# First queries before the second batch's divisors, one set-up product moved, and shift and scale read from DRAM in a four-layer kernel

## The chip, the cores and the metric

The kernel runs on one core of one Trainium2 chip. The metric is the device time of one execution in microseconds (us), as the median of several runs; lower is better. Before the change it is 702.77 us (median of 6 runs, 702.45 to 706.2).

## The reference

The input x has 8 batches of 256 tokens of 256 features; a condition vector of 64 numbers belongs to each batch. Four layers follow one another, each added to its input:

```python
x = x + L0(x, cond)   # norm scaled by cond, 16-head attention, norm, SwiGLU of width 1024
x = x + L1(x, mask, cond)
x = x + L2(x, cond)   # quaternion rotation of the features
x = x + L3(x, cond)   # router, top 2 of 8 experts, each three matmuls 256-512-512-256

# L1, after its attention:
out = out @ Wo.T
xn  = out / sqrt(mean(out*out) + EPS) * rms_scale
mod = silu(cond) @ Wc.T + bc            # 8 x 512
shift, sc = split(mod, 2)
xn  = xn * (1 + sc) + shift
```

The change touches the condition's part of L1 (`mod`) and the order of the first rounds. All numbers are float32.

## The kernel before, in words

**Staging.** The kernel works batch by batch. An attention of one layer and one batch is four *blocks*: `Attention.scores` does eight matrix instructions into `s` (L988, one buffer of four PSUM banks, `ps_s` with `bufs=1`) and one exponential on ACT, `pe` (L990). So the scores of a block cannot start before the exponential of the block before has read `s`. `values` (L1001) multiplies the exponentials with the values. Blocks are taken from a fixed `queue`, first those of layer L0 for batches 0, 1 and 2, then L1 and L0 in turn. Between blocks, `run` puts *pieces*: projections, SwiGLU products, transposes. All of these write to the pool `ps_m` (function `bank`), which has three buffers.

**What sets the order.** TensorE, VectorE and ScalarE take their instructions in the order of the Python text (`manual_schedule`); in the first stage, up to the six rounds of `run("bbbbbb", ...)`, GpSimd does too. SyncE, which issues most transfers, and GpSimd in the later stages are ordered by a planner. So where a function is called in the text is where its instructions stand in each engine's queue.

**The start.** `first_norm(b)` (through `normed`) takes the sums of squares of a batch on ACT (L878), then eleven small VectorE operations for the reciprocal root (`rsqrt`, L619 to L624, the "divisors"), then scales the tokens (`xs`, L900, on ACT for batches 0 and 1). `first(b)` transposes `xs` on TensorE and applies the condition's scale and shift on VectorE (`conditioned`, L924, giving `xT`), then projects keys (`pk`, L932, copied by ACT to `kT`), queries (`pq`, L932, scaled by VectorE to `qz`, L946, two instructions) and values (`pv`, L954, copied by ACT to `va`, L957). `prepare_condition` (L692 to L696) and `prepare_router` (L750 to L758) are eight short VectorE instructions and one on ACT; the first of them, `keyseen` (L692), reads the mask `maskT`, which GpSimd's queue loads fourth, behind `WcT`, `bc_b` and `rs_b`. `set_up_condition` multiplies silu(cond) with `WcT` (`pmod`, L715) into `mod_all`, 8 batches on 8 partitions, and GpSimd writes that to the DRAM tile `mod_rows` (L719). `set_up_router` is one more small product (`pgconst`, L763).

**The set-up in the six rounds.** `second_step` is a generator that is advanced once at the end of each of rounds 1 to 5. It interleaves `set_up_rotation` with the third batch's `first_turned(3)` and the norm `n2` of batch 1. `first_turned` sends its reciprocal roots through DRAM (`rstd_rows`, L1063) and back on all partitions (`rb`, L1065), and VectorE multiplies by them (`xr`, L1071). `set_up_rotation` makes, in its four steps: `rotg` and `gall`; then `coef`, `pmc` (L833, `mod` once more, now with features on partitions, from `silu_c` and `WcT`), from it `mc` (L834, L835) and `scaled` (L839); then the products `phall` (L847) and `pshift` (L854) with their readers `hall` (L851) and `each` (L856); and last `pshg` (L862) and its copy `shg` (L863).

Of the kernel before, what the change touches and what calls it, by code (L numbers as in the profile page):

```python
# [12 lines left out]
ALU = mybir.AluOpType  # L13
# [3 lines left out]
P = 128  # L17
B, S, D = 8, 256, 256
# [3 lines left out]
E, M = 8, 512  # L22
KC = D // P
# [11 lines left out]
WROW = B3O + D  # L35

SMALL = dict(condT=B, qrT=4, sgT=1, affb=4 * KC, rms=KC, wg=KC * E, ggw=E, wgb=E, ggb=E,
             wg4=4 * E, rms4=4, bcc=2 * KC, rsc=KC)

SL = 256  # L40

# [452 lines left out]
def block_kernel(ctx: ExitStack, tc: tile.TileContext, a: dict, out: bass.AP):  # L494
    nc = tc.nc
# [57 lines left out]
    def scales():  # L553

        nc.vector.tensor_scalar(pbit, pidx, DH, None, ALU.bitwise_and)
        nc.vector.tensor_copy(pbitf, pbit)
        nc.vector.tensor_scalar(par[:, 0:1], pbitf, -0.25 / DH, 0.25, ALU.mult, ALU.add)
        nc.vector.tensor_scalar(par[:, 1:2], pbitf, 0.25 / DH, None, ALU.mult)
# [12 lines left out]
    part, at = {}, 0  # L571
# [118 lines left out]
    def prepare_condition():  # L690

        nc.vector.tensor_scalar(keyseen, maskT8[:, :, 0], -1.0, 1.0, ALU.mult, ALU.add)  # L692

        nc.scalar.activation(tanh_c, condT[0:C, :], AF.Tanh, scale=0.5)
        nc.vector.tensor_scalar(half_c, condT[0:C, :], 0.5, None, ALU.mult)
        nc.vector.scalar_tensor_tensor(silu_c, tanh_c, 1.0, half_c, ALU.add, ALU.mult)  # L696
# [15 lines left out]
    def set_up_condition():  # L712

        pm = bank("pmod", (B, 2 * D))
        nc.tensor.matmul(pm, silu_c, wcT, start=True, stop=True)  # L715
        mod = wt("oT", [B, 2 * D], "mod_all")
        nc.vector.tensor_tensor(mod, pm, bc_b, ALU.add)
        nc.vector.scalar_tensor_tensor(mod[:, D:], mod[:, D:], 1.0, rs_b, ALU.add, ALU.mult)
        nc.gpsimd.dma_start(out=mod_rows, in_=mod)  # L719
        yield 0.4  # L720

    def set_up_slots():
# [81 lines left out]
    def set_up_rotation():  # L804
        prepare_rotation()

        nc.vector.tensor_tensor(
            wg4s, part["wg4"].rearrange("p (j e) -> p j e", e=E),
            part["rms4"].unsqueeze(2).to_broadcast([P, 4, E]), ALU.mult,
        )  # L810
        for h in range(2):
            r = slice(h * C, (h + 1) * C)
            nc.vector.tensor_copy(rmine[r], rotg[r].rearrange("p j (k h) -> p k h j", h=2)[:, :, h, :])
        turned = work.tile([P, KC, 4, E], F32, tag="raw", bufs=2, name="turned")
        nc.vector.tensor_tensor(
            turned, rmine.unsqueeze(3).to_broadcast([P, KC, 4, E]),
            wg4s.unsqueeze(1).to_broadcast([P, KC, 4, E]), ALU.mult,
        )
        nc.vector.tensor_reduce(gall, turned.rearrange("p k j e -> p k e j"), AX.X, ALU.add)
        nc.vector.tensor_copy(wv1[:, :, D:], gall)  # L820

        nc.sync.dma_start(out=coef_row, in_=rotg[0:C].rearrange("c j i -> c (j i)"))
        rows_in = wt("x4", [P, C, 4, 4], "coef_in", 1)
        nc.sync.dma_start(
            out=rows_in.rearrange("p c j i -> p (c j i)"),
            in_=coef_row.rearrange("c w -> (c w)").partition_broadcast(P),
        )
        yield
        nc.gpsimd.tensor_copy(coef, rows_in.rearrange("p c j i -> p i j c"))

        pm = bank("pmc", (P, 2 * KC, B))
        for k in range(2 * KC):
            nc.tensor.matmul(pm[:, k, :], wcT[:, k * P : (k + 1) * P], silu_c, start=True, stop=True)  # L833
        nc.vector.tensor_tensor(mc, pm, part["bcc"].unsqueeze(2).to_broadcast([P, 2 * KC, B]), ALU.add)  # L834
        nc.vector.scalar_tensor_tensor(  # L835
            mc[:, KC:], mc[:, KC:], 1.0, part["rsc"].unsqueeze(2).to_broadcast([P, KC, B]), ALU.add, ALU.mult
        )
        scaled = wt("mod", [P, KC, B, E], "scaled")
        nc.vector.tensor_tensor(  # L839
            scaled, mc[:, KC:].unsqueeze(3).to_broadcast([P, KC, B, E]),  # L840
            gall.unsqueeze(2).to_broadcast([P, KC, B, E]), ALU.mult,
        )
        yield
        ph = bank("phall", (P, KC, B * E))
        for c in range(KC):
            for k in range(KC):
                nc.tensor.matmul(  # L847
                    ph[:, c, :], wo1n[:, k, c * P : (c + 1) * P], scaled[:, k].rearrange("p b e -> p (b e)"),
                    start=k == 0, stop=k == KC - 1,
                )  # L850
        nc.vector.tensor_copy(hall.rearrange("p k b e -> p k (b e)"), ph)  # L851
        ps = bank("pshift", (B, E))
        for k in range(KC):
            nc.tensor.matmul(ps, mc[:, k, :], gall[:, k, :], start=k == 0, stop=k == KC - 1)  # L854
        each = work.tile([B, B, E], F32, tag="r_each", bufs=1, name="each")
        nc.vector.tensor_tensor(  # L856
            each, ps.unsqueeze(1).to_broadcast([B, B, E]),
            ident[0:B, 0:B].unsqueeze(2).to_broadcast([B, B, E]), ALU.mult,
        )
        yield  # L860
        pb = bank("pshg", (P, B * E))
        nc.tensor.matmul(pb, ones[0:B, :], each.rearrange("p b e -> p (b e)"), start=True, stop=True)  # L862
        nc.vector.tensor_copy(shg.rearrange("p b e -> p (b e)"), pb)  # L863
        yield
# [5 lines left out]
    def bank(name, shape=(P, 2, S)):  # L870
        return ps_m.tile(list(shape), F32, tag="m", name=name)
# [165 lines left out]
    def do(parts):  # L1037
        for _ in parts:
            pass
# [5 lines left out]
    def first_norm(b):  # L1045
        s = state[b]
        s["x"] = xs_in.pop(b)
        yield from normed(
            lambda xs: s.update(xs1=xs), s["x"], f"n1_{b}", nc.gpsimd if b > 1 else nc.scalar,
            (nc.scalar, nc.scalar if b else nc.vector),  # L1050
        )
# [700 lines left out]
    def chain(*gens):  # L1752
        for g in gens:
            yield from g
# [33 lines left out]
    def once(f, *args):  # L1788
        f(*args)
        yield  # L1790

    def at_once(*gens):
        for g in gens:
            for _ in g:
                pass
        yield
# [10 lines left out]
    with tc.manual_schedule(engines=by_text):  # L1807
        unread = ps_o.tile([P, P], F32, tag="o", name="unread")
        keep_busy(9)
        n1 = first_norm(0)  # L1810
        next(n1)
        next(n1)
        set_up_factors(0)
        set_up_factors(2)
        do(n1)
        keep_busy(3)
        g0 = first(0)
        next(g0)
        keep_busy(2)
        scales()  # L1820
        n1 = first_norm(1)
        next(n1)
        next(n1)
        next(g0)
        next(g0)
        do(n1)
        do(g0)
        blank = set_up_slots()
        prepare_condition()
        cond_g = prepare_router()  # L1830
        finish_slots(*blank)
        def third(b):

            operand = first(b)
            yield next(operand)
            yield from set_up_router(cond_g)
            yield from operand

        def take(n, pieces):
            for _ in range(n):  # L1840
                yield next(pieces)


        operands = first(1)
        run("b", chain(take(1, operands), set_up_condition(), set_up_router(cond_g)), 9.0, rest=False)
        run("b", take(1, operands), 9.0, {0: [once(prepare_quaternions)]}, rest=False)
        n1 = first_norm(2)
        run("b", iter(()), 0.0, {0: [n1]})
        run("b", operands, 9.0, {0: [at_once(n1)]}, rest=False)
        operands = first(2)  # L1850
        then = run("b", iter(()), 0.0, hold=True)
        run("b", take(1, operands), 9.0, owed=then, soon=1, rest=False)

        def second_step():
            rotation = set_up_rotation()
            next(rotation)
            yield
            n1 = first_turned(3)
            next(n1)
            yield  # L1860
            n2 = in_parts(1, "n2")
            next(n1)
            next(n2)
            next(rotation)
            yield
            do(n1)
            next(n2)
            next(rotation)
            set_up_ones()
            yield  # L1870
            do(n2)
            yield from rotation

        set_up = second_step()
        gaps = [1.9, 5.0, 7.2, 7.2, 7.2, 7.2]
        run("bbbbbb", chain(operands, others(0)), gaps, {n: [set_up] for n in range(1, 6)}, soon=2)
    by_text = {mybir.EngineType.DVE, mybir.EngineType.Activation}
    text_order = ctx.enter_context(ExitStack())
    text_order.enter_context(tc.manual_schedule(engines=by_text))
# [231 lines left out]
```

## Time and profile before

| what | value |
|---|---|
| median of 6 runs | 702.77 us |
| profiled execution | 703.18 us |
| its span on the core | 701.4 us |
| granted TensorE clock, mean | 0.995 |
| PE busy | 687.2 us, 98% |
| DVE busy | 365.8 us, 52% |
| ACT busy | 255.5 us, 36% |
| POOL busy | 180.3 us, 26% |
| DMA, slices 0 to 2 of 40 | 8, 4 and 1 tenths busy |

PE is TensorE, DVE VectorE, ACT ScalarE, POOL GpSimd, SP SyncE. The profile is one execution; its time lies 1.8 us above its span. The first two of forty slices (17.5 us each) are the only early ones in which the transfers fill the queues: the weights of the first layers arrive there. A chain of waits, followed back from the last instruction, names at each time the work that set the end.

### The profile page before, as it was taken

To read this page: it belongs to the slowest core of one execution; us is meant where nothing else is said; L and a number is where in the kernel's file an instruction comes from. 1 tells how busy PE (TensorE), PEld (TensorE's weight loads), DVE (VectorE), ACT (ScalarE), POOL (GpSimd) and SP (SyncE) were. 2 spreads that over 40 slices of the span, in tenths; PEclk is the share of its full clock that TensorE was granted. 3 is DMA by queue.
4 is the path that set the end of the run, shared out by engine and by line. 5 is a ranking of instruction groups with operands and counts; after the bars stand their busy time and mean duration, and the time that the engine had idled before them with its cause. 6 is when DMAs were issued, how large, how long until landed. Compare 5 with 4: busy or idle time off the path is not lost.

```text
span 701.4 us, 11187 instructions
## 1 busy us (share of the span) xinstructions
PE 687.2 (98%) x4258; PEld 530.8 (76%) x4258; DVE 365.8 (52%) x1165; ACT 255.5 (36%) x411; POOL 180.3 (26%) x223
## 2 busy tenths in 40 slices
PE   8999999999999999999999999999999999999995
PEld 7567776767667667766666786688888998999894
DVE  4664354584488576477675676688222222222221
ACT  4664243544454444354443235332111222221220
POOL 5501500000000231000320016224373432443213
PEclk9999999999999999999999999999999999999998
DMA  8410201002011001020000051746595866676712
GB/s 301 152 61 17 38 1 38 16 1 39 16 61 39 1 17 8 6 71 1 9 9 1 17 204 18 301 139 208 145 312 158 231 238 180 174 268 195 250 24 29
DMA packets 28879, 70.01 MB, mean 100 GB/s; under 512 B 9033, under 2 KB 22225, under 8 KB 26385
## 3 DMA queue, kind: packets, MB, share of 16 engines
q1 hardware_dynamic: 20032, 57.70, 25.2%
q0 software_dynamic: 8496, 11.32, 7.4%
q8 instruction: 35, 0.57, 0.3%
q14 instruction: 28, 0.22, 0.1%
q10 hardware_dynamic: 288, 0.18, 0.1%
HBM read 59.67 MB, written 9.53 MB: 99 GB/s over the span
## 4 chain that ended last, share of the span: by engine, by line
PE 90%; DVE 5%; ACT 2%; DMA 1%; issue 1%; SPq 0%; POOL 0%; POOLq 0%; DVEq 0%; ACTq 0%
PE ph_a_rest L1528 10%; PE s_a L988 9%; PE pd L1141 8%; PE pg L1128 8%; PE ph_a_p L1528 7%; PE ph L1128 7%; PE o_a L1001 7%; PE ph_s_sure L1528 6%; PE pe_a_rest L1558 3%; PE pq_a L932 3%; PE pk_a L932 3%; PE pe_a_p L1558 3%; PE py L1024 2%; PE pe_s_sure L1558 2%; PE pv_a L954 2%; PE py L1174 2%
## 5 line engine op out<-in xcount | busy, mean ns | idle before, releaser
L990 ACT ACTIVATE pe_a<-s_a 128x2048 f32<-128x2048 f32 x64 | 120.1, 1876 | 101.0 <-PE s_a L988 100.9
L988 PE MATMUL s_a<-qz_a,kT_a 32*128 32x512 f32 x512 | 73.0, 640 | 3.0 <-DVE xg L1159 0.9
L1001 PE MATMUL o_a<-pe_a,va 128*32 128x256 f32 x1024 | 61.9, 382 | 0.0
L1128 PE MATMUL pg<-xT_n,gate_wT 128*128 128x256 f32 x256 | 61.8, 385 | 0.0
L1128 PE MATMUL ph<-xT_n,hid_wT 128*128 128x256 f32 x256 | 61.6, 384 | 0.0
L1001 PEld LDWEIGHTS o_a<-pe_a,va 128*32 128x32 f32 x1024 | 30.0, 110 | 39.8 <-issue 23.4
L1141 PE MATMUL pd<-out_wT,hT 128*128 128x256 f32 x256 | 59.7, 385 | 0.4 <-DVE hT L1136 0.4
L1141 PEld LDWEIGHTS pd<-out_wT,hT 128*128 128x128 f32 x256 | 47.4, 190 | 13.7 <-issue 4.0
L1128 PEld LDWEIGHTS ph<-xT_n,hid_wT 128*128 128x128 f32 x256 | 47.7, 190 | 13.2 <-DVE rq_v_n L619 2.3
L1128 PEld LDWEIGHTS pg<-xT_n,gate_wT 128*128 128x128 f32 x256 | 47.6, 190 | 11.9 <-issue 3.6
L1010 DVE STREAM_TRANSPOSE tu_a<-o_a 128x512 f32<-128x512 f32 x32 | 22.8, 712 | 52.3 <-PE o_a L1001 52.3
L1528 PE MATMUL ph_a_rest<-h_a_rest,w_a_rest 128*128 128x256 f32 x224 | 49.6, 380 | 0.0
L1528 PEld LDWEIGHTS ph_a_rest<-h_a_rest,w_a_rest 128*128 128x128 f32 x224 | 42.1, 190 | 5.4
L1101 POOL TENSOR_TENSOR xy<-y,x 128x512 f32<-128x512 f32 x8 | 10.1, 1268 | 139.3 <-DVE rq_v_r L619 55.0
L1539 DVE TENSOR_SCALAR h_a_rest<-ph_a_rest,w_a_rest 128x256 f32<-128x256 f32 x28 | 13.5, 484 | 57.3 <-PE ph_a_rest L1528 56.3
L1316 POOL DMA_INDIRECT slots<-rec,posi x32 | 31.8, 994 | 22.1 <-issue 7.6
L988 PEld LDWEIGHTS s_a<-qz_a,kT_a 32*128 32x128 f32 x512 | 20.1, 183 | 22.2 <-issue 13.1
L1134 DVE SCALAR_TENSOR_TENSOR sg<-th,pg 128x512 f32<-128x512 f32 x32 | 21.9, 685 | 28.4 <-ACT th L1132 28.3
L1528 PE MATMUL ph_a_p<-h_a_p,w_a_p 128*128 128x192 f32 (+2 forms) x224 | 36.0, 319 | 0.0
L1132 ACT ACTIVATE th<-pg 128x512 f32<-128x512 f32 x32 | 19.0, 594 | 46.4 <-PE pg L1128 46.4
L1537 ACT ACTIVATE h_a_rest<-ph_a_rest,w_a_rest 128x256 f32<-128x256 f32 x28 | 13.2, 473 | 60.7 <-DVE h_a_rest L1539 60.7
L1528 PEld LDWEIGHTS ph_a_p<-h_a_p,w_a_p 128*128 128x128 f32 x224 | 34.9, 191 | 0.1
(351 smaller groups left out, 1177.7 us busy)
## 6 DMA issues: line engine op xcount, KB each, us to landing
w_a_rest<-in_experts SPq DMA_DIRECT2D x7, 2180.0 KB, 9.5
w_a_p<-in_experts SPq DMA_DIRECT2D x7, 2180.0 KB, 9.2
w_s_sure<-in_experts SPq DMA_DIRECT2D x4, 2180.0 KB, 10.1
w_s_early<-in_experts SPq DMA_DIRECT2D x1, 2180.0 KB
mod<-mod_rows SPq DMA_DIRECT2D x8, 256.0 KB, 3.3
tokens<-x SPq DMA_DIRECT2D x4, 512.0 KB, 3.8
out<-x SPq DMA_DIRECT2D x4, 512.0 KB, 4.9
x<-in_x SPq DMA_DIRECT2D x7, 256.0 KB, 2.7
```

The lines of the kernel that those rows point to most:

```text
L932: nc.tensor.matmul(pp[:, c, :], w[:, k, c * P : (c + 1) * P], xT[:, k, :], start=k == 0, stop=k == KC - 1)
L988: nc.tensor.matmul(sc[:, j], kT[r, c, kc * P : (kc + 1) * P], qz[r, c], start=True, stop=True)
L990: nc.scalar.activation(pe, sc, AF.Exp)
L1001: nc.tensor.matmul(o[32 * i : 32 * i + 32, qd, :], va[:, kc, 8 * c + 4 * qd + i].rearrange("p a d -> p (a d)"), pe[:, 2 * qd + i // 2, i % ...
L1010: nc.vector.transpose(turned.rearrange("p q j a d -> p (q j a d)"), o.rearrange("p q s -> p (q s)"))
L1128: nc.tensor.matmul(ps[:, j, :], w[:, k, o : o + P], yT[:, k, :], start=k == 0, stop=k == KC - 1)
L1132: nc.scalar.activation(th, pg, AF.Tanh, scale=0.5)
L1134: nc.vector.scalar_tensor_tensor(sg, th, 1.0, pg, ALU.add, ALU.mult)
L1141: nc.tensor.matmul(pd[:, t, :], hT[:, c, t * P : (t + 1) * P], out_w[:, c, :], start=c == 0, stop=c == HID // P - 1)
L1316: sc = nc.gpsimd.indirect_dma_start(out=slots, out_offset=bass.IndirectOffsetOnAxis(ap=posi[:, t : t + 1], axis=0), in_=rec[:, t, :], in_o ...
L1528: nc.tensor.matmul(ph[:, c - c0, 0:many], w[:, o : o + P], src[:, k, 0:many], start=k == 0, stop=k == n_in - 1,)
L1558: nc.tensor.matmul(pos[q][0:p, q, :], h2[:, k, q * p : (q + 1) * p], w[:, o : o + D], start=k == 0, stop=k == MC - 1,)
```

## The change

Three edits, all before the steady rounds:

```diff
 SMALL = dict(..., wg4=4 * E, rms4=4
-             , bcc=2 * KC, rsc=KC)
+             )
...
 def set_up_condition():
...
         nc.gpsimd.dma_start(out=mod_rows, in_=mod)
+
+        for j in range(2 * KC):
+            nc.sync.dma_start(out=mc[:, j, :], in_=mod_rows[:, j * P : (j + 1) * P].rearrange("b p -> p b"))
         yield 0.4
...
 def set_up_rotation():
...
-        pm = bank("pmc", (P, 2 * KC, B))
-        for k in range(2 * KC):
-            nc.tensor.matmul(pm[:, k, :], wcT[:, k * P : (k + 1) * P], silu_c, start=True, stop=True)
-        nc.vector.tensor_tensor(mc, pm, part["bcc"]..., ALU.add)
-        nc.vector.scalar_tensor_tensor(mc[:, KC:], mc[:, KC:], 1.0, part["rsc"]..., ALU.add, ALU.mult)
         scaled = wt("mod", [P, KC, B, E], "scaled")
...
         scales()
+        prepare_condition()
+        cond_g = prepare_router()
         n1 = first_norm(1)
-        next(n1)
         next(n1)
         next(g0)
         next(g0)
-        do(n1)
+        next(n1)
         do(g0)
         blank = set_up_slots()
-        prepare_condition()
-        cond_g = prepare_router()
         finish_slots(*blank)
...
-        run("b", chain(take(1, operands), set_up_condition(), set_up_router(cond_g)), 9.0, rest=False)
-        run("b", take(1, operands), 9.0, {0: [once(prepare_quaternions)]}, rest=False)
+        run("b", chain(set_up_condition(), set_up_router(cond_g)), 9.0, {0: [at_once(n1)]}, rest=False)
+        run("b", take(2, operands), 9.0, {0: [once(prepare_quaternions)]}, rest=False)
...
         def second_step():
...
             next(rotation)
             set_up_ones()
             yield
+            next(rotation)
+            yield
             do(n2)
-            yield from rotation
...
-        run("bbbbbb", ..., {n: [set_up] for n in range(1, 6)}, soon=2)
+        run("bbbbbb", ..., {n: [set_up] for n in range(1, 6)}, soon=2, starts={5: [set_up]})
```

First, the eight small VectorE instructions of the condition and the router come ahead of everything of batch 1, and batch 0's `qz` comes ahead of batch 1's eleven divisors. Batch 1's `xs` moves behind the first block, and its transposes, `xT` and `pk` stand together between the second and the third block; before, the transposes and `xT` stood between the first and the second. Second, `pmc` and its two VectorE readers are gone; four transfers by SyncE fill `mc`, each reading 128 features of all 8 batches from `mod_rows`, single 4-byte numbers that lie 2 KB apart, to 128 partitions. Third, `pshg` and `shg` stand at the start of round 5, right behind that round's scores, and no longer at its end; `n2`'s last step stays at the end.

## The prediction

> **What bounds the kernel.** I read the page first: engine shares and the chain that ended last.
>
> ```profile
> PE 687.2 (98%) x4258; PEld 530.8 (76%) x4258; DVE 365.8 (52%) x1165; ACT 255.5 (36%) x411; POOL 180.3 (26%) x223
> ...
> PE 90%; DVE 5%; ACT 2%; DMA 1%; issue 1%; SPq 0%; POOL 0%; POOLq 0%; DVEq 0%; ACTq 0%
> ```
>
> TensorE sets the time. Of its 14 us of idling, some 7 lie behind its last matmul; the view of waits finds about 5 us before that, 3 of them in the first 90 us, where all three edits lie. So a microsecond won or lost there should arrive at the end whole: behind 92 us the chain is PE almost throughout. Next I read the chain of waits in order of time up to 140 us (start, duration, what).
>
> ```profile
> 11.13 0.52 ACT junk_n L878 x2
> ...
> 13.81 1.32 DVE qz_a L946 x2
> 15.13 0.07 DVE keyseen L692
> ...
> 15.28 1.17 PE s_a L988 x8
> 16.45 0.02 issue
> 16.47 1.89 ACT pe_a L990
> 18.36 0.04 issue
> 18.40 1.19 PE s_a L988 x8
> ...
> 64.27 0.99 PE pmc L833 x8
> ...
> 76.13 0.18 PE pshift L854 x4
> 76.31 1.07 PE s_a L988 x8
> ...
> 82.76 0.36 PE pshg L862 x2
> 83.12 0.60 PE pt_x L888 x4
> 83.72 0.02 issue
> 83.74 0.59 ACT x2T L1154
> ```
>
> Up to 15.28 the chain runs over batch 1's squares and divisors to batch 0's `qz`: that is what the first edit attacks. Then scores and exponential alternate every 3.13 us (15.28, 18.40, 21.54, 24.68). `pmc` stands in the chain with 0.99, and behind `pshg` the chain leaves PE for `x2T`. Last, the timeline, for what the chain does not name.
>
> ```profile
> 5.06 0.77 POOL L525 DMA_DIRECT2D maskT<-in_maskT  x1
> ...
> 11.04 1.89 PE L932 MATMUL pq_a<-xT_n,L_WqT 128*128 128x256 f32 x8
> ...
> 17.04 1.00 DVE L924 TENSOR_SCALAR xT_n<-pt_n,aff 128x256 f32<-128x256 f32 x2 [0.60 <-PE pt_n L888]
> ...
> 74.76 0.69 DVE L1071 TENSOR_TENSOR xr<-xr,rb 128x512 f32<-128x512 f32 x1 [3.92 <-DMA rb<-rstd_rows]
> ...
> 78.02 0.20 DVE L856 TENSOR_TENSOR each<-pshift,ident 8x64 f32<-8x64 f32 x1
> ```
>
> **Edit 1, the start.** `pq` ends at 11.04 + 1.89 = 12.93, so `qz` can start at 12.98 where it started at 13.73. Its two instructions take 1.40, to 14.38. PE has `pv` until about 14.5 (its 12.76 start plus the usual 1.73), so the first scores go at 14.50, not 15.28: 0.78 won. The eight small instructions, 15.05 to 16.10 in the trace or 1.05 in all, move into the idle 2.03 us that DVE had before the divisors, behind 9.64; they are hidden if `maskT` has landed by 12.98 - 1.05 = 11.9. Its landing is not shown. `bc_b`, the same queue's load two ahead, landed 4.7 us after its issue, which gives 9.8; the slowest of that queue's early transfers (`out<-zero`, 256 KB) took 6.7, which gives 11.8. I take 9.8, the nearest row, and nothing for it. `keyseen` ran unheld at 15.05, so that is the ceiling.
>
> Now what comes behind. Scores 14.50, exponential 15.69 to 17.58, second scores 17.62: still 0.78 ahead. In between PE has only `pmod` and `pgconst` (1.02 + 0.43). The divisors run 14.4 to 16.5, and `xs` (0.91 on ACT) behind the exponential, to 18.5, under the second scores. Before, transposes and `xT` were done under the first exponential, and `pk` (19.47, 1.93 to the next PE work) filled the second. Now all three stand behind the second scores: transposes at 17.62 + 1.07 = 18.69, first half of `xT` 0.69 later (16.35 to 17.04 in the trace) and 0.55 long, `pk` at 19.98. PE idles 0.7 there and about as long before the second scores. Third scores at 19.98 + 1.93 = 21.91, fourth at 25.04, against 24.68: **0.4 us lost**. If `pk` needs both halves of `xT`, 0.8. If `pk` should not hold the third scores, 0.8 is won. I take 0.4: batch 0's `pk` started at 9.20, when only one half (8.60 to 9.15) was done.
>
> **Edit 2, `mc`.** `pmc` leaves PE: **-0.99**, the chain's row. The two DVE instructions (0.18 + 0.17) lay in DVE time that now becomes waiting: nothing. Added are four SP transfers, at the trace's 0.32 to 0.47 an issue. They wait for `mod_rows`, which the first load of `mod` (26.12) waited for too; with its DVE producers 0.5 later, say 26.6. Queued behind them on SP are that load (read at 84.87) and batch 3's `x` and `xT` (38.15 and 38.63, waiting for a buffer): nothing is late as long as the four end before 38. 4096 pieces of 4 bytes have no like here. Below: a `trec` load, 256 pieces of 16 bytes, landed in 1.8 us at best, so 16 times that in a row is 29 us, landing by 56. Above: `rb`, 128 pieces, took 4.3 us; its engines were busy about 2.6 us for 8 pieces each (0.33 us a piece), which for 256 each is 84 us, landing near 111. The `trec` row is nearest in size. `scaled` is due at 67.7, so I take nothing; the lower bound is hidden with 11 us to spare, the upper is not.
>
> A rule speaks against this edit. The Trainium skill, "DMA: Bandwidth & Descriptors", section "Rules for kernel authors", says that a non-contiguous last dimension becomes one descriptor per element, and puts a rearranged plain transfer at 19 times a hardware transpose. As an estimate from that page, 19 times the 3.3 us in which a `mod` load landed is 63 us, a landing near 89 and some 22 us lost; by the `trec` row the sum has no such term, and I follow the row.
>
> **Edit 3, `pshg`.** Its 0.36 is the same in either place, but it needs `each`. DVE reaches `each` only behind `xr` (held to 74.76 by `rb`), eleven divisors and `hall`: done at 78.22, 78.27 on PE. PE without `pmc` stands at `pshg` at 77.38 - 0.99 = 76.39: **a new wait of +1.9**. `rb` starts from divisors that follow PE's `pg` ahead of `pmc`, so the whole chain shifts with edit 1 and 1.9 holds. Behind it wait the last quarter of `pd`, then `pk`, `pq`: all of PE. In return, `pv` no longer stands behind `pshg` and `pt_x`: of three `ps_m` buffers, `pshg` held one there; now `pk`'s is free. From `pt_x` to `pv` it was 1.26, elsewhere transposes take 0.44 to the next PE work (88.10 to 88.54): **-0.8**. If `pv` waits as before, 0; if `each` came in time, the +1.9 would be 0.
>
> A rule again: "TensorE: Matmul & The Clock Gate", Part 1, has the clock halve after an idle window of about 3.4 us. The row is the granted clock, 1.00 in every 2 us up to 100, also where PE idled 0.6 of 2 us. By the rule 1.9 us alone would cost nothing; one of 3.4 us would, and the sum would gain about 1.7.
>
> **Sum:** +0.4 - 1.0 + 1.9 - 0.8 = **+0.5 us**. On the profiled execution: span 701.4 to 701.9, time 703.2 to 703.7. On the median, 0.4 below that execution: 702.77 + 0.5 = **703.3 us**, no change that can be told: 0.3% (2.1 us) is about what a measurement of this kernel can tell from none.
>
> **Rivals.**
> *The mask holds the queries* (slower). From a landing at 11.9 on, every microsecond delays `qz`. Against: both neighbours of that load say 9.8 to 11.8. For: transfers fill the queues up to 24 us. At the ceiling `keyseen` runs at 15.05, `qz` ends at 17.5, first scores 17.55, and the same steps bring the fourth to 28.1: 3.4 lost, not 0.4. That is 706.3.
> *`mc` late* (slower). From 67.7 on DVE stands at `scaled`, and `tu`, `hT` and so `pd` behind it. A landing at 72 costs 72 - 67.7, some 4 us: 707.6; at the upper bound of 111 it would be 43, or 746, to which I give no more than 0.02. The `rb` row speaks for it, the `trec` row against.
> *The lead stays and nothing stalls* (faster). `pk` does not hold the third scores and `each` comes in time: -0.8 - 1.0 - 0.8 = -2.6, 700.2. Against: the text order of DVE, which puts `xr` ahead of `each`. Without the stall alone: +0.5 - 1.9, 701.4.
> *The queues are planned anew.* SP everywhere and POOL in the later stages are not in text order, and three buffers of `ps_m` are dealt out afresh. For: POOL's `xT_n` (1.1 for two) waited 41.1 us in all behind others. If in three rounds it stands behind one more `xs` of 1.27, 3.8 is lost: 707.1. Gains are bounded by the few microseconds of PE waits left: a case of -2.5, 700.8 with the sum.
>
> **Chances.** Forecast 0.46; no stall alone 0.08 (both within). Mask 0.12, of which 0.08 beyond 0.3%. `mc` 0.08, of which 0.06 beyond. Lead kept 0.07, faster. Queues 0.19, of which 0.13 slower and 0.06 faster. In all: faster 0.13, same 0.60, slower 0.27. **Range** 700.8 to 706.6: the mask's ceiling, the single lost stall and part of the queues; about 0.1 stays out on each side. The forecast's own range is 702.1 to 704.5 (`pv` not gained +0.8, both halves +0.4; upper sizes of the gains below).
>
> **What would show it.** Right: first scores near 14.5, `keyseen` not waiting; `pk` of batch 1 behind the second scores with PE idle 0.6 before it, fourth scores near 25.0; no `pmc`; `mc` landed before 56 and no wait at `scaled`; PE waiting about 1.9 for `each` ahead of `pshg`; `pv` 0.44 behind `pt_x`; from 92 on the same steps some 0.5 later. Wrong: `keyseen` held by a transfer, DVE held at `scaled`, no wait at `pshg`, or a difference that appears behind 92 us.

## The result and the profile after

| | before | after |
|---|---|---|
| median | 703.24 us (67 runs, 702.19 to 706.63) | 707.51 us (30 runs, 704.03 to 713.55) |
| profiled execution | 703.18 us | 710.14 us |
| its span | 701.4 us | 708.4 us |

The changed kernel is slower: ratio 1.0058, with a 95% interval of 1.0045 to 1.0072. Forecast were 703.3 us and a range of 700.8 to 706.6, so the median lies 0.9 us above the range. One thing must be known before the spans are compared: in some executions of the kernel before, and of most others here, the matrix work of the first 12 us runs at half pace, which makes an execution some 3.3 us longer; the profile after is of such an execution and the one before is not, so what follows compares steps and not spans.

TensorE sets the end of the changed kernel as it did before. From its page, the engines' busy time and their shares of the chain:

```profile
PE 692.8 (98%) x4250; PEld 535.1 (76%) x4250; DVE 365.7 (52%) x1163; ACT 255.4 (36%) x411; POOL 180.2 (25%) x223
...
PE 90%; DVE 6%; ACT 1%; DMA 1%; issue 1%; POOL 0%; POOLq 0%; DVEq 0%; ACTq 0%
```

Eight matrix instructions fewer (`pmc`), yet PE is busy 5.6 us longer. Work that is less and takes longer has been slowed, so the durations in the chain are the next thing to read. The chain of waits of the changed kernel (start, duration, what):

```profile
5.71 3.51 PE paff L636 x16
...
12.50 2.59 PE pk_a L927 x8
15.10 1.73 PE pq_a L927 x8
...
18.55 1.11 PE s_a L983 x8
...
21.62 1.14 PE s_a L983 x8
22.76 0.60 PE pt_n L883 x4
23.38 0.56 DVE xT_n L919
23.98 2.01 PE pk_a L927 x8
26.00 1.11 PE s_a L983 x8
...
29.06 1.14 PE s_a L983 x8
...
74.91 4.30 DMA rb<-rstd_rows
79.23 0.69 DVE xr L1066
...
82.57 0.13 DVE each L851
82.75 0.69 PE pshg L857 x2
83.43 3.71 PE pd L1136 x8
87.14 2.81 PE pk_a L927 x8
89.96 1.73 PE pq_a L927 x8
91.69 0.44 PE pt_x L883 x4
92.12 1.73 PE pv_a L949 x8
```

Three things are to be seen. `paff` takes 3.51 us at the start (1.88 in a trace with the start alone, further down): the half pace of the first 12 us, which has nothing to do with the change. Behind the second scores stand `pt_n`, `xT_n` and `pk` in one row, as forecast. And behind `pshg` eight `pd` products take 3.71 us and eight `pk` products 2.81. In the chain before, the same products, and `pv`, took:

```profile
77.38 1.93 PE pd L1141 x8
79.30 1.73 PE pk_a L932 x8
...
84.38 1.99 PE pv_a L954 x8
```

The view of PE's waits names one new one, its cost in total, count and longest:

```profile
PE pshg L857 <- DVE each L851: 2.0, 1, 2.0
```

The windows of 2 us of the changed kernel give, behind the window and its length, the busy time and instructions of each engine (PE, PEld for its weight loads, DVE, ACT, POOL), then the granted TensorE clock, the DMA share and GB/s:

```profile
80.00:82.00 2.00, 0.78 (x8) 0.00 (x0) 1.70 (x9) 1.16 (x1) 1.90 (x3) 1.00 0.55 120
82.00:84.00 2.00, 1.25 (x4) 1.04 (x5) 0.87 (x5) 0.72 (x1) 1.90 (x3) 0.60 0.53 142
84.00:86.00 2.00, 2.00 (x6) 1.64 (x5) 0.00 (x0) 0.00 (x0) 2.00 (x2) 0.50 0.00 0
86.00:88.00 2.00, 2.00 (x6) 1.56 (x5) 0.69 (x1) 0.00 (x0) 1.91 (x3) 0.50 0.00 0
88.00:90.00 2.00, 2.00 (x7) 1.64 (x7) 0.00 (x0) 0.00 (x1) 2.00 (x2) 0.70 0.02 4
90.00:92.00 2.00, 2.00 (x13) 1.76 (x12) 0.28 (x1) 1.38 (x3) 0.61 (x1) 1.00 0.00 0
```

In shorter windows the granted clock falls to 0.50 at 82.4, while PE still waits, and is back at 89.2: six products in 2 us instead of eleven. In the trace before it is 1.00 in all of these windows. The 7.0 us between the spans are then, from the steps of the two chains:

| step | us |
|---|---|
| `pq` starts at 15.10, not 11.04 (half pace, not of the change) | +4.1 |
| `pq` to fourth scores: 13.96, not 13.64 | +0.3 |
| fourth scores to the place of `pmc`: 39.60, not 39.59 | 0.0 |
| `pmc` gone | -1.0 |
| wait for `each` | +2.0 |
| `pshg`, `pd`, `pk` at half clock: 7.21, not 0.36 + 1.93 + 1.73 | +3.2 |
| `pt_x` to the end of `pv`: 0.44 + 1.73, not 1.26 + 1.99 | -1.1 |
| behind that | -0.5 |

The row "behind that" is 608.95 us from the scores near 99 to the end, against 609.43 before; in ten traces, these two and eight of the runs below, it lies between 608.9 and 609.7, so nothing of the change is seen there.

### The profile page after: what moved, and what is told of

Same layout as the page of the kernel before. It is cut to its first block, busy times and chain, and to the rows that moved or that the text cites. A ratio compares the mean times of both kernels' runs of the same rounds, so it can differ in the third digit from the quotient of the medians.

```text
span 708.4 us, 11172 instructions
## 1 busy us (share of the span) xinstructions
PE 692.8 (98%) x4250; PEld 535.1 (76%) x4250; DVE 365.7 (52%) x1163; ACT 255.4 (36%) x411; POOL 180.2 (25%) x223
## 2 busy tenths in 40 slices
DMA packets 33039, 70.02 MB, mean 99 GB/s; under 512 B 13193, under 2 KB 26385, under 8 KB 30545
## 4 chain that ended last, share of the span: by engine, by line
PE 90%; DVE 6%; ACT 1%; DMA 1%; issue 1%; POOL 0%; POOLq 0%; DVEq 0%
PE ph_a_rest L1523 10%; PE s_a L983 9%; PE pg L1123 8%; PE ph_a_p L1523 7%; PE pd L1136 7%; PE o_a L996 7%; PE ph L1123 7%; PE ph_s_sure L1523 6%; PE pk_a L927 4%; PE pq_a L927 3%; PE pe_a_rest L1553 3%; PE pe_a_p L1553 3%; PE pv_a L949 2%; PE py L1019 2%; PE pe_s_sure L1553 2%; PE py L1169 2%
## 5 line engine op out<-in xcount | busy, mean ns | idle before, releaser
L1136 PE MATMUL pd<-out_wT,hT 128*128 128x256 f32 x256 | 61.5, 392 | 0.4 <-DVE hT L1131 0.4
```

The lines of the kernel that those rows point to most:

```text
L1136: nc.tensor.matmul(pd[:, t, :], hT[:, c, t * P : (t + 1) * P], out_w[:, c, :], start=c == 0, stop=c == HID // P - 1)
```

## The experiments

My theory was now that the first two edits do what was worked out, and that the third costs its wait and, on top of it, a stretch of half clock. Rivals: the start costs more than 0.4 to 0.5 (its new gaps lower the clock, or the half-paced start comes more often), `mc` costs something, or it is chance. The four kernels of the first set are compared with 35 runs of the kernel before, median 703.09 us, on the same chip.

**The whole change without its third edit.** `pshg` is back at the end of round 5.

```diff
-            next(rotation)
-            yield
             do(n2)
+            yield from rotation
...
-        run("bbbbbb", ..., soon=2, starts={5: [set_up]})
+        run("bbbbbb", ..., soon=2)
```

> The changed kernel with pshg put back to the end of round 5 (edit 3 undone; edits 1 and 2 stay). Theory, the clock: the loss of some 4 us is the 2.0 us wait for each and the half clock that follows it (pshg, pd and pk together 7.2 us instead of 4.0), so both go: before + 0.5 (start) - 1.0 (pmc), about 0.5 us below before, and granted clock 1.00 from 70 to 100 us. Rival, the start: edit 1 makes the first 12 us run at half pace (paff 3.5 us instead of 1.95 in the profile of the changed kernel), 3.3 us; then this run stays about 3 us above before.

Measured: 703.35 us, ratio 1.0003 (0.9981 to 1.0025). The clock is 1.00 in every window from 80 to 88 and the mean granted clock of its runs 0.9965, as before; after the change it is 0.9928 on average. So the loss goes with the third edit; the interval leaves 1.3 us below to 1.8 us above before. The gain of 0.5 that the other two should leave is not seen in the median, nor excluded. Part of the reason stands in its chain: `pk` behind `pd` starts at 82.50, when `each` is done, and takes 1.97, not 1.73. It reads nothing of `each`; the link that the source offers is a `ps_m` buffer, which `pshift` holds until `each` has read it. `each` delays PE also where `pshg` doesn't wait for it.

**The first edit alone.** Of the diff only the order in the start, with `pmc` and `pshg` as before.

```diff
+        prepare_condition()
+        cond_g = prepare_router()
         n1 = first_norm(1)
...
-        do(n1)
+        next(n1)
         do(g0)
...
-        run("b", take(1, operands), ...)
+        run("b", take(2, operands), ...)
```

> The kernel before with edit 1 alone. Theory, the clock: the profile of the changed kernel has 10.51 us from the first to the fourth scores against 9.40, and 0.7 less from pq to the first scores, so +0.4 to +0.5 us against before, and the half pace of the first 12 us comes up about as often as in before (18 of its 67 runs lie at 706). Rival, the start: +3 us or more in most runs.

Measured: 704.56 us, ratio 1.0023 (1.0001 to 1.0045), mean clock 0.9964 against 0.9965. The chain of this kernel, with a start at full pace:

```profile
5.60 1.88 PE paff L636 x16
...
11.20 1.73 PE pq_a L932 x8
...
14.65 1.11 PE s_a L988 x8
...
17.72 1.14 PE s_a L988 x8
...
20.09 2.02 PE pk_a L932 x8
22.10 1.12 PE s_a L988 x8
...
25.17 1.14 PE s_a L988 x8
```

First scores at 14.65 (forecast 14.50), fourth at 25.17 (forecast 25.04, before 24.68): +0.49. The two new gaps of PE of 0.6 and 0.7 us don't lower the clock in this trace. The median says +1.5 with an interval that reaches from 0.1 to 3.2 us; that the edit costs more than its 0.5 is neither shown nor excluded.

**The second edit alone.** `pmc` and its two readers leave, the four transfers come in.

```diff
+        for j in range(2 * KC):
+            nc.sync.dma_start(out=mc[:, j, :], in_=mod_rows[...].rearrange("b p -> p b"))
...
-        pm = bank("pmc", (P, 2 * KC, B))
-        for k in range(2 * KC):
-            nc.tensor.matmul(pm[:, k, :], wcT[:, k * P : (k + 1) * P], silu_c, ...)
```

> The kernel before with edit 2 alone: mc read from DRAM, no pmc. Theory: PE has 1.0 us less to do, and with pmc out of the chain the time is 1.0 us below before; the four transfers land by 35 us, 2.9 us after their issue, and nobody waits for them. Rival, late mc: the transfers, or the loads queued behind them on SP, hold DVE at scaled or delay batch 3, and the time is not below before.

Measured: 704.41 us, ratio 1.0012 (0.9992 to 1.0032). In the trace, fourth scores to the scores near 92 take 66.65 instead of 67.37: -0.72, not -0.99. The missing 0.3 is at `pk`, as in the run above. From this trace's timeline (start, duration, engine, line, operation, tiles):

```profile
81.33 0.20 DVE L851 TENSOR_TENSOR each<-pshift,ident 8x64 f32<-8x64 f32 x1
...
81.55 1.97 PE L927 MATMUL pk_a<-xT_n,L_WkT 128*128 128x256 f32 x8
```

`each` ends at 81.54 in the chain and `pk` starts at 81.55: 0.04 behind the end of `pd`, and its 1.97 is 0.24 more than the 1.73 that it took without a wait. PE is early by `pmc`'s 0.99, `each` isn't. The transfers themselves cost nothing. In the trace of the whole change the transfer view has, per transfer, 4.0 KB and 2.9 us from issue to landing, and SP's timeline their issues:

```profile
mc<-mod_rows SPq DMA_DIRECT2D x4, 4.0 KB, 2.9
```

```profile
28.79 2.62 SPq L722 DMA_DIRECT2D mc<-mod_rows  x4
```

Four issues of 0.65 us, landed by about 34, more than 30 us before `scaled` reads them at 72.

**The third edit alone.**

```diff
+            next(rotation)
+            yield
             do(n2)
-            yield from rotation
```

> The kernel before with edit 3 alone: pshg behind the scores of round 5, pmc still on PE. Theory, the clock: PE reaches pshg at 77.4 and each is ready at 78.2, so PE waits 0.9 us, not 1.9, and wins 0.8 at pv: about the time of before if 0.9 us of idling leaves the clock at 1.00, and up to 3.2 us more if it halves as in the changed kernel. So this run says whether 0.9 us is enough to halve the clock. Rival, the start: no difference of either sign beyond 0.3 us, clock 1.00.

Measured: 706.32 us, ratio 1.0037 (1.0016 to 1.0059): slower. The wait is 0.9, as expected with `pmc` still ahead of it:

```profile
78.72 0.43 PE L862 MATMUL pshg<-each,ones 8*128 8x64 f32 x2 [0.88 <-DVE each L856]
```

Its trace has clock 1.00 behind the wait, yet the mean clock of its runs is 0.9955 instead of 0.9965, which is 0.7 us of 703. Six of the twelve lie at 0.995 or less (three of the 35 of before). In this trace, one of the six, the low clock stands at 8.0 to 11.4 and behind the last product; where it stands in the other five no trace shows. A second trace of the same kernel has 702.61 us, a wait of 1.2 and clock 1.00 behind it again:

> Edit 3 alone once more, for a second trace: PE waits 0.9 us for each. Theory: in some five of twelve executions of the first series the mean clock was 0.993 to 0.995 and the time 705 to 708.6, so this trace shows half clock behind the wait with a chance of about 0.4; otherwise it is as the first trace. Rival: the wait is 0.9 us and the clock stays at 1.00 in any case.

So no half clock was seen behind a wait of 0.9 or 1.2 us; the wait, `pv`'s gain of 0.8 and the clock give +0.8 of the 3.2 us between the medians (whose interval reaches down to 1.1). The rest stays open; half-paced starts may be part of it, since eight of the twelve runs took more than 705 us, and ten of the 35 of before.

**The wait filled or removed.** If the clock falls because PE stands still, then work in the gap keeps it, though the wait stays; if `pshg`'s place does it, nothing changes. And if `each` comes early, wait and half clock go together. First six, then eight products of the identity matrix with itself, which nobody reads, between the scores of round 5 and `pshg`; then, without these, one exchange of two lines in round 4, which puts `hall` and `each` right behind `xr` in VectorE's order, ahead of the eleven divisors.

```diff
+            idle = ps_o.tile([P, P], F32, tag="o", name="idle")
+            for _ in range(6):
+                nc.tensor.matmul(idle, ident, ident, start=True, stop=True)
             next(rotation)
```

```diff
             do(n1)
-            next(n2)
             next(rotation)
+            next(n2)
             set_up_ones()
```

> The changed kernel with six products of the identity with itself (nobody reads them) put into PE's order between the scores of round 5 and pshg: about 1.9 us of work in the time in which PE waits for each. Theory, the clock: the wait for each stays as it is, but PE is not idle in it, so the clock stays at 1.00 and pshg, pd and pk take 4.0 us, not 7.2: lower by 1.5 to 3.3 us than the changed kernel, to about before + 0.5. Rival, the wait alone: each is as late as before, so nothing is won or the time gets longer by what the six products overrun.

> The changed kernel with one swap in second_step: the step with phall, hall, pshift and each comes ahead of batch 1's eleven divisors, not behind them. Theory: each is ready about 2.2 us earlier on DVE, before PE reaches pshg, so neither the wait nor the half clock come up: the start's +0.5 to +0.9, pmc's -1.0 and pv's -0.8 remain, 1 us below before. Rival, the place of pshg costs by itself (the three buffers): PE waits elsewhere and the time stays above before.

> The kernel before with edits 2 and 3 and the same swap, without edit 1: the parts that should win. Theory: -1.0 (pmc) - 0.8 (pv), and no wait of pk for each, which edit 2 alone had (its trace has pk 0.3 us late): 1.8 us below before. Rival: the wins are below what can be measured, ratio 1.000.

> The changed kernel itself, beside the three others on one chip. Theory, the clock: about 3 to 5 us above before, clock 0.5 behind the wait for each in the trace, for how long depends on the run; all other steps as in its first trace. Rival, the start: a trace with a fast start and no half clock behind round 5 is at before + 3 nevertheless.

In this set every kernel, the one before too (728.74 us, 35 runs), takes about 25 us more; in the traces of the four PE waits longer at three places between 200 and 500 us, up to 6.7 us, and their first 100 us go as in the other sets.

| kernel | median, us | ratio to before (95%) | mean clock |
|---|---|---|---|
| before | 728.74 | | 0.9827 |
| the change again | 731.88 | 1.0048 (1.0025 to 1.0070) | 0.9786 |
| the change, wait filled with six | 730.22 | 1.0010 (0.9987 to 1.0033) | 0.9812 |
| the change, `each` earlier | 727.68 | 0.9992 (0.9969 to 1.0015) | 0.9817 |
| edits 2 and 3, `each` earlier, old start | 728.16 | 0.9984 (0.9965 to 1.0003) | 0.9822 |

The change is slower here by the same ratio, and 0.0041 of mean clock is 3.0 us of 732: nearly the whole loss. With `each` earlier the loss is gone, and `pshg` follows the scores at once:

```profile
75.93 1.07 PE s_a L983 x8
77.00 0.15 PE pshg L857 x2
77.15 1.93 PE pd L1136 x8
```

The profiled execution of the change in this set was its fastest (727.97), and its trace is the one of three that has the wait and not the half clock:

```profile
78.00:80.00 2.00, 0.77 (x4) 0.68 (x5) 1.26 (x8) 1.20 (x1) 1.90 (x2) 1.00 0.65 193
80.00:82.00 2.00, 2.00 (x11) 1.77 (x10) 0.31 (x1) 0.00 (x0) 2.00 (x3) 1.00 0.00 0
```

PE is busy 0.77 of 2 us as in the first trace, but the next 2 us hold eleven products at clock 1.00. The wait doesn't bring the half clock every time.

The edges of the clock tell more. In this trace it also falls to 0.50 within each of the three later waits, of 3.7, 2.5 and 6.7 us, for 6.8 us each time, and once behind the last product. Read from windows of 0.5 us, the seven edges, from 255.4 to 719.6, lie 0, 2, 32, 34, 55, 57 and 136 steps of 3.41 us behind the first. Counted back, such a step ends at 77.9, inside the wait for `each` (77.3 to 79.2): 0.65 us of the wait lie in one step and 1.32 in the next. In the first trace the step that ends with the fall, at 82.4, holds 1.6 us of it. With each trace cut into its own steps, behind the first 12 us and in all fourteen traces, no step in which PE stood still for less than 1.5 us ends in a fall; of six between 1.5 and 1.9 three do, and all from 2.0 on do. So what a wait costs hangs on how these steps divide it; no run moved the wait against them. The pace of the start goes with the steps, too: counted back to the first microseconds, a step ends between -0.1 and 0.5 us in the seven traces with the half-paced start, the first of the change among them, and between 1.2 and 2.8 in the seven others, this one among them.

A third set, against 23 runs of the kernel before with median 706.04 us (13 of these had the half-paced start, more than usual), took eight identity products, to cover the whole wait, and repeated the two edits with `each` earlier. One more trace of the changed kernel was to say whether the first was typical.

> The changed kernel with eight products of the identity in the wait for each, not six: 2.1 us of work against a wait of 2.0, so that PE doesn't idle there at all (six left 0.3 us). Theory, the clock: mean granted clock as in before (six products left it 0.0015 below before, the changed kernel is 0.004 below), and the time at before + 0.5 to + 1. Rival: the clock halves in spite of the filling, because such products or the short ones before them don't count; the time stays 2 us or more above before.

> Edits 2 and 3 with each made earlier, without edit 1, a second series of the version that came out lowest (ratio 0.9984). Theory: 1.8 us of PE time less than before, ratio 0.9975 to 0.9985 once more, PE without a wait at pshg, pk or pv. Rival: its first series was luck in how often the first 12 us ran at half pace; ratio 1.000.

> The changed kernel once more, for a third trace: a wait of 2.0 us for each as in the two before. Theory: the half clock behind it begins at a time that has nothing to do with the kernel's own steps and lasts a multiple of about 3.4 us (6.8 in the first trace, none in the second).

With eight products: 704.74 us, ratio 1.0007 (0.9988 to 1.0026), mean clock 0.9964 against 0.9967; one of the twelve runs has 0.994 or less, of the changed kernel's 32 recorded executions 28 have. PE's timeline of this kernel (each product is recorded as two instructions of `idle`):

```profile
76.09 1.14 PE L983 MATMUL s_a<-qz_a,kT_a 32*128 32x512 f32 x8
77.16 2.05 PE L1867 MATMUL idle<-ident 128*128 128x128 f32 x16
79.49 0.43 PE L857 MATMUL pshg<-each,ones 8*128 8x64 f32 x2 [0.27 <-DVE each L851]
79.85 1.99 PE L1136 MATMUL pd<-out_wT,hT 128*128 128x256 f32 x8
```

`pshg` is as late as in the changed kernel, 3.4 us behind the start of the scores (there 3.1), but PE stood still for only 0.27 of it, and `pd` takes 1.99. That separates the two losses: useless products in the gap bring the mean clock back, while the time of the gap itself is still spent.

The third trace of the changed kernel: 710.87 us, wait 2.0, clock 0.62 in the window from 82, 0.50 from 84 to 88 and 0.68 from 88: the first trace again, to a tenth of a microsecond. So of three traces two have the half clock for 6.8 us and one has none. In both the clock comes back after two steps and falls again 182 steps behind its first fall. The steps lay alike in these two, which both have the half-paced start, so they can't show what the expectation says of the time at which it begins.

**The version that comes out lowest.** Edits 2 and 3 with `each` earlier and the old start: 701.18 us, ratio 0.9950 (0.9932 to 0.9968) against the kernel before. Some of this is chance, since only 3 of its 12 runs had the half-paced start; among the executions of both kernels without it the medians are 700.93 and 703.09, 2.2 us apart. Its chain has no step that waits for `each`:

```profile
78.34 1.07 PE s_a L983 x8
79.41 0.19 PE pshg L857 x2
79.60 1.92 PE pd L1136 x8
81.52 1.73 PE pk_a L927 x8
```

In the set of the table above the same kernel won 0.6 us, within its interval. That it is faster than the changed kernel is clear (728.16 against 731.88 there, and 701.18 against the 707.51 of the first comparison); by how much it beats the kernel before, 0.6 to some 2 us, is not.

## Why the prediction was wrong

**The step that failed** is the wait of +1.9 in edit 3: the sum took it at its own length, with no term for the clock behind it, nor a bound for one. The reason stands in the paragraph behind it, "By the rule 1.9 us alone would cost nothing", together with the row it was set beside, clock 1.00 also where PE idled 0.6 of 2 us. That row says nothing of a gap three times as long. The wait came at 2.0 us (forecast 1.9), and in two of the three traces the clock behind it was 0.50 for 6.8 us, which cost 3.2 us. The Trainium skill, "TensorE: Matmul & The Clock Gate", Part 1, puts an idle window of about 3.4 us ahead of the half clock. The length agrees with the steps of 3.41 us above, but here 1.6 us of standing still within a step were enough, and the measurement decides. Ahead of the gap, from 78.5 to 80.8, PE had only small products: `phall` with 64 columns, `pshift` with 8 and scores on 32 partitions. Whether these count as idle was not tried. The same section says that the window runs freely, and that the number of slow products at a kernel's start therefore changes from run to run; that agrees with a wait that the steps cut at one place in two traces and at another in the third. Over its recorded executions the mean clock of the changed kernel is 0.9928 against 0.9965: about 2.6 us of 703, and with the forecast's +0.5 that gives 3.1 of the 4.3 us between the medians. It is no rare case: 28 of the 32 lie at 0.994 or less, and twelve of these took 705.1 to 706.5 us, too short for a half-paced start as well. The rest may be the start (more half-paced starts, or the unsettled part of edit 1) and was not settled.

**Edit 1** was right in its steps, by the trace of the first edit alone: first scores 0.63 earlier, `pk` behind the second scores with PE idle 0.6, fourth scores +0.49 (forecast +0.4). `keyseen` ran unheld at 12.22 in the changed kernel's trace, so the rival *the mask holds the queries* is out.

**Edit 2** was right for the whole change, -0.99 with `mc` landed by about 34, 22 us ahead of the `trec` bound of 56. Following that row and not the rule of 19 times was right; the Trainium skill, "DMA: Bandwidth & Descriptors", section "Rules for kernel authors", sets its 19 against a hardware transpose, which the `mod` load that the estimate multiplied is not. What it says of one descriptor per element agrees with this case: on the two pages of the profile, packets under 512 bytes rise from 9033 to 13193, by 4160, and the four transfers hold 4096 elements. Even the row was far too long, since 1024 pieces of 4 bytes landed in 2.9 us where 256 pieces of 16 bytes had taken 1.8. So *`mc` late* is out. What I missed is that `pk`, too, waits for `each`, by the source through the buffer of `pshift`: without edit 3 the gain is 0.7.

**Edit 3**: the wait 2.0 for 1.9, `pv` 0.8 earlier as forecast, and 0.26 more because its products no longer start behind a wait. Its own terms were right to a few tenths; the clock behind it wasn't among them.

***The queues are planned anew*** did not show: behind the scores near 92 to 99 the traces differ by less than 0.8 us in all, with no step of the change in it. ***The lead stays and nothing stalls***: the version with `each` earlier has no stall, and its 1.1 us below before lie within the interval; it needs VectorE's order, which this change left as it was.

## What to carry to other kernels

A wait of 2 us on the engine that sets the time may be followed by a loss larger than itself, so a forecast that adds such a wait needs a term for the clock behind it, with zero as its lower end and half of the slowed stretch (here 6.8 us) as its upper. Before a consumer is moved ahead on one engine, look at what stands ahead of its producer on the other: here two exchanged lines on VectorE removed wait and half clock together. A buffer that is shared by rotation can hold an instruction that reads nothing of the late producer; `pk` behind `each` is such a case, as far as the source and the chain tell.

## What the hardware showed unexpectedly

A gap of 2.0 us on TensorE, after some 2 us of small products, was followed by a granted clock of 0.50 for 6.8 us in two of three traces. Gaps of 0.6 to 0.9 us and one of 1.2 were not, and unread products in the gap kept the clock. The edges of the clock lie on steps of 3.41 us within a trace, and it fell at the end of steps in which PE had stood still for 1.6 us or more, not of those with less than 1.5. In 18 of 67 runs of the kernel before, by their times over 705 us, the first 12 us ran at half pace. The seven traces that show such a start (`paff` 3.51 us) have a granted clock of 1.00 in every window up to 26 us, so the record of the clock doesn't hold it. The trace of the third edit alone shows another thing: `paff` at 1.98, then a clock of 0.50 from 8.0 to 11.4 us though PE is busy throughout, and first scores at 15.80, not 14.65 to 15.28. Transfers of 1024 single 4-byte numbers, 2 KB apart, landed 2.9 us after issue and took SyncE 0.65 us each to issue.
